# Sums on POOL in SBUF in place of identity products on PE, and norm statistics from ACT's copy, in a hybrid state-space and attention block

## The chip, the cores and the metric

One NeuronCore of a Trainium2 chip. The metric is the device time of one launch in microseconds: 11580.11 us, the median of 3 runs (11578.98 to 11580.71).

## What is computed

The input x is 8 images of 64 x 64 tokens with 96 channels, float32. Per image, cut to what matters here:

```python
x = x + ss2d(group_norm(x))                  # layer 0
t = t + attn(layer_norm(t))                  # layer 1: linear attention, N = 4096 tokens
t = t + ffn(layer_norm(t))                   # 96 -> 384 -> 96, fp8 products
# ss2d:
xh, z = split(x @ in_proj.T)                 # 192 + 192 channels
xc = silu(conv3x3(xh))
s0, s1 = xc[diag], xc[anti]                  # the tokens along two sorts of diagonals
xs = [s0, s1, reversed(s0), reversed(s1)]    # four directions
h  = h * exp(delta * A) + (delta * u) * B    # a scan over 4096 positions, 16 states n
y  = sum over n of h * C   (+ D * u)
y01 = ys[0:2] + reversed(ys[2:4])            # an end's two directions: forward plus backward
y   = y01[0][inv_diag] + y01[1][inv_anti]    # the two pairs
out = (layer_norm(y) * ln_w + ln_b) * silu(z) @ out_proj.T
```

Two sums of this are what the change is about: that of forward and backward direction (line `y01`), and that of the two pairs, diagonal and antidiagonal (the line after it).

## The kernel before, in words

**The scan.** An image is walked in 16 steps m: first pair of directions (q = 0, forward, both diagonals at once in the halves of the 128 partitions), 8 chunks of T = 512 positions, then the backward pair (q = 1), 8 chunks. A step has 16 iterations i, one for each state n; 2048 iterations in all, written out as one loop in `run`. In iteration i the engines get, each in its own order:
- ACT: `decay(i+2)` (exp, L985), jobs, `times_b(i+2)` (feedT, L1007; for one state in sixteen POOL does it, L998);
- DVE: `recur(i)`: in the five "D" states three multiplications of feed with du (L1032), then three scans (L1028), jobs between the second and the third;
- PE, in three parts: `turn(i+1)` (L1015, L1017) into the three PSUM banks `feed`, a third of `reduce(i-4)` (L1061, transposes of h that add up over the 16 states in the PSUM tile y), jobs;
- POOL: `keep(i-1)` (L1042) and `read(i-1)` (h times C, L1047), jobs;
- SP issues all DMAs in order; `fetch(i+4)` (L976) brings a C row, cc, into one of five buffers.

h has six buffers, decay three, feedT two, each feed bank one. POOL may thus be up to some three iterations behind before PE's `reduce` needs it.

**The sum of the directions.** `place(m)`, three iterations into step m+1, copies y to SBUF (ys) by ACT. For q = 0 this is one copy (L1089) and a DMA to `part` in DRAM. For q = 1 the part of the same chunk is fetched at the step's start (y0, a tile that shares its one buffer with ys, L1056), added by three PE products with the identity into y after states 8, 9 and 10 (L1074), and y then goes by two copies (L1094), one per diagonal, and eight DMAs (L1104) to `wide`, an array in DRAM from which rows of tokens can be read.

**The prologue** of step m+2 (an urgent job, L900 to L957) starts in iteration 13 of step m: products for dt, B and C, softplus (L942, with two table loads), then du = delta x u on POOL (L947, iteration 3 of step m+1), its 12 transposes on PE (L953) and three copies duT on ACT (L955). du has two buffers.

**Jobs.** What is not scan is written as Python generators: each `yield` names the engine of the next piece (act, dve, gp for POOL, pe, or bank, which also asks for one of two PSUM banks), its planned us, and a lag. `Work.at` is called at fixed places of the iteration and takes the pieces that are due, as far as a credit per engine allows; urgent jobs come first and may overdraw. The table LAGS says how many iterations after the last piece a piece is due, by the pair of engines: ACT to DVE (AV) 1, POOL to DVE (GV) 1, POOL to PE (GP) 1 and the last part. A lag in the yield replaces it: `dve(1.0, 0)` puts DVE's piece into the same iteration. Placement is fixed when the program is made; on the chip each engine runs its queue in order and waits on semaphores.

While image b is scanned, jobs do the front of image b+1 (norm, convolution: steps 0 to 5; walk: 5 to 7) and the tail of image b-1: `join` for 8 groups of 512 tokens (steps 7 to 11), `attention`, `layers` for 8 groups (12 to 15). The last image's tail stands alone at the end (`last`).
- `join(c)` loads the two pairs' rows ys[0], ys[1] from `wide`; adds them by PE products with the identity into a bank (L665), which ACT copies to yn (L672) and DVE takes the norm statistics of (L675, L676); norm, transposes, times the gate, out projection into a bank po, ACT's copy t (L708), statistics of po (L713), normed xa on POOL, its Gram matrix and transposes. At most three joins are open, and join c's sum waits for join c-2's end. In the last tail DVE adds (L656) and takes statistics from SBUF (L658).
- `layers(c)`: the same pattern with po, the copy t (L809) and statistics (L813), then the two fp8 products.

At iteration LAG + 1 = 5 of an image all jobs must be out (`work.finish(all_done)` issues what is left with no scan between), and the next image's jobs start.

Of the kernel before, what the change touches and what calls it, by code (L numbers as in the profile page):

```python
# [9 lines left out]
F32 = mybir.dt.float32  # L10
# [25 lines left out]
G = 3  # L36
# [579 lines left out]
def tail(tc, work, x, out, k, at, b, last=False):  # L616
# [4 lines left out]
    with tc.tile_pool(name=f"t1_{b}", bufs=1, **area) as p1:  # L621
# [5 lines left out]
        with tc.tile_pool(name=f"t2_{b}", bufs=8 if last else 2, **area) as p2:  # L627
# [3 lines left out]
            def join(c):  # L631
# [22 lines left out]
                if last:  # L654
                    yield dve(2.5)
                    nc.vector.tensor_tensor(yn, ys[0], ys[1], ALU.add)  # L656
                    for i in range(4):
                        nc.vector.bn_stats(st[:, i, :], yn[:, i, :])  # L658
                        nc.vector.bn_aggr(mv[:, i, :], st[:, i, :])
                for j in range(0 if last else 2):  # L660
                    ps = yield bank(0.65)
                    v = view(ps, P, 2, DI)
                    for i in range(2):
                        for d in range(2):
                            nc.tensor.matmul(  # L665
                                v[:, i, :], k.ident, ys[d][:, 2 * j + i, :],
                                start=(d == 0), stop=(d == 1), skip_group_check=True,
                            )
                        if i == 0:
                            yield pe(0.65)  # L670
                    yield act(0.5)
                    nc.scalar.copy(yn[:, 2 * j : 2 * j + 2, :], v)  # L672
                    yield dve(1.0, 0)
                    for i in range(2):
                        nc.vector.bn_stats(st[:, 2 * j + i, :], v[:, i, :])  # L675
                        nc.vector.bn_aggr(mv[:, 2 * j + i, :], st[:, 2 * j + i, :])  # L676
                    work.release(ps)
                r, m = yield from rsqrt(nc, p2, k, mv, P, 4, "n")
                yield act(1.4)
                for i in range(4):  # L680
# [27 lines left out]
                nc.scalar.copy(t, po)  # L708
                if not last:
                    nc.sync.dma_start(out=at.mid[:, s, :], in_=t)  # L710
                yield dve(1.7, 0)
                for i in range(4):
                    nc.vector.bn_stats(st[:, i, :], po[:, i, :])  # L713
                    nc.vector.bn_aggr(mv[:, i, :], st[:, i, :])
                work.release(ps)
                r, m = yield from rsqrt(nc, p2, k, mv, P, 4, "a")
                xa = ys[0].rearrange("p a c -> p (a c)")[:, 0 : 4 * (DM + 1)].rearrange("p (a c) -> p a c", a=4)
                yield gp(1.6)
# [64 lines left out]
        with tc.tile_pool(name=f"t3_{b}", bufs=8 if last else 3, **area) as p2:  # L783

            def layers(c):
# [22 lines left out]
                yield act(0.5)  # L808
                nc.scalar.copy(t, po)  # L809
                st, mv = tile("st", [P, 4, 6]), tile("mv", [P, 4, 2])  # L810
                yield dve(1.7, 0)
                for i in range(4):
                    nc.vector.bn_stats(st[:, i, :], po[:, i, :])  # L813
                    nc.vector.bn_aggr(mv[:, i, :], st[:, i, :])
                work.release(ps)
                r, m = yield from rsqrt(nc, p2, k, mv, P, 4, "f")
                xf = tile("xf", [P, 4, DM])
                yield gp(1.4)
# [41 lines left out]
def run(tc, psum, dram, x, out, w, NB):  # L860
# [39 lines left out]
    def prologue(m):  # L900
# [42 lines left out]
        w.tables()  # L943
        o.delta = delta
        yield gp(3.4)
        du = o.du = tile("du", [P, G, T])
        nc.gpsimd.tensor_tensor(du, delta, u, ALU.mult)  # L947
        duT = tile("duT", [P, TB * G, P])
        for j in range(G):
# [9 lines left out]
    def bring(m):  # L959

        b, q, c = steps[m]
        work.finish(lambda: c in image(b).walked)
        u = pool.tile([P, G, T], F32, tag="u", name=f"u_{m}", bufs=2)
        made[m] = SimpleNamespace(u=u, c={})
        for d in range(2):
            nc.sync.dma_start(
                out=u[d * GC : (d + 1) * GC],
                in_=image(b).seq[d][:, c * T : (c + 1) * T].rearrange("(g i) t -> i g t", i=GC),
            )
# [49 lines left out]
    def recur(i):  # L1019
        m, n = divmod(i, NS)  # L1020
        _, q, _ = steps[m]
        h = hs[i] = pool.tile([P, G, T], F32, tag="h", name=f"h_{i}", bufs=6)
        a = decays.pop(i)
        back = slice(None, None, -1) if q else slice(None)

        def scan(g):
            init = carry[m - 1][:, n, g : g + 1] if m % NST else 0.0
            nc.vector.tensor_tensor_scan(h[:, g, back], a[:, g, back], feed[g][:, back], init, ALU.mult, ALU.add)  # L1028

        if FEED[n] == "D":  # L1030
            for g in (1, 2, 0):
                nc.vector.tensor_tensor(feed[g], feed[0], made[m].du[:, g, :], ALU.mult)  # L1032
        scan(0)
        scan(1)
        work.at("V")
        scan(2)
# [12 lines left out]
    def reduce(i, part):  # L1049
        m, n = divmod(i, NS)  # L1050
        b, q, c = steps[m]
        if n == 0 and part == 0:
            sums[m] = psum.tile([P, TB * G, P], F32, tag="y", name=f"y_{m}")
            if q:
                other[m] = pool.tile([P, TB * 2 * DI], F32, tag="ys", name=f"y0_{m}")
                nc.sync.dma_start(out=other[m], in_=image(b).part[:, c, :])  # L1056
        y = sums[m]
        some = range(4 * part, 4 * part + 4)
        for j in some:
# [5 lines left out]
        if q and n in (1, 2, 3) and part == 2:  # L1065
            for j in range(4 * (n - 1), 4 * n):
# [2 lines left out]
                    y[:, j, :], made[m].u[:, g, r * P : (r + 1) * P], w.skip[:, g, :],  # L1069
                    start=False, stop=False, skip_group_check=True,  # L1070
                )
        if q and n in (8, 9, 10) and part == 2:
            j = n - 8
            nc.tensor.matmul(  # L1074
                y[:, 4 * j : 4 * j + 4, :].rearrange("p a c -> p (a c)"), w.ident,
                other[m][:, j * T : (j + 1) * T], start=False, stop=False, skip_group_check=True,
            )
        if part == 2:
            hs.pop(i)

    def place(m):

        b, q, c = steps[m]
        y = sums.pop(m)
        ys = pool.tile([P, TB * 2 * DI], F32, tag="ys", name=f"ys_{m}")
        if q == 0:
            nc.scalar.copy(ys, y.rearrange("p j c -> p (j c)"))  # L1089
            nc.sync.dma_start(out=image(b).part[:, c, :], in_=ys)  # L1090
            return
        rows = ys.rearrange("p (d k c) -> p d k c", d=2, k=TB)
        for d in range(2):
            nc.scalar.copy(  # L1094
                rows[:, d].rearrange("p k (g i) -> p k g i", i=GC),
                y.rearrange("p (k g) (d i) -> p d k g i", g=G, d=2)[:, d],
            )
            stride = (3 * WW + 1) * DI if d == 0 else (3 * WW - 1) * DI
            for v in range(2):
                for again in range(2):  # L1100
                    first = (c * (T // HH) + v + (again + d) * WW) * DI
                    view = image(b).wide[d][first : first + HH * stride].rearrange("(h x) -> h x", x=stride)
                    view = view[:, 0 : TB * 2 * DI].rearrange("h (k x) -> h k x", k=TB)[:, :, 0:DI]
                    nc.sync.dma_start(out=view, in_=rows[v * HH : (v + 1) * HH, d])  # L1104

    def begin(b):
        return front(tc, work, x, w, image(b), b)
# [61 lines left out]
    for i in range(total + LAG + 1):  # L1169
        m, n = divmod(i, NS)  # L1170
        b, at = divmod(i, PER)
        if i < total:
            if at == LAG + 1 and b:
                work.finish(all_done)
                work.stream(between(b))
            if at == PER // 2 and b + 2 < NB:
                work.stream(before(b + 2))
            if n == NS - 3 and m + 2 < len(steps):
                work.start(prologue(m + 2), urgent=True)
            if n == NS // 2 and m + 2 < len(steps):  # L1180
                bring(m + 2)
# [22 lines left out]
        if i + 4 < total:  # L1204
            fetch(i + 4)
        feeds.pop(i, None)

    work.finish(all_done)
    scans.close()
# [82 lines left out]
```

## Time and profile before

| what | value |
|---|---|
| runs, median of 3 | 11580.11 us |
| profiled execution | 11584.24 us, span 11582.5 us |
| mean granted TensorE clock | 0.913 |
| DVE scans L1028, 128x512 | 6144, 1263 ns (with carry) |
| POOL read L1047, 128x1536 | 2048, 3455 ns |
| POOL du L947, 128x1536 | 128, 3445 ns |
| PE L665 (a join's sum) | 896, 351 ns, busy 182.4 us |
| PE L1074 (a step's sum) | 384, 595 ns, busy 196.9 us |
| ACT copies L672, L1089, L1094 | 469, 1416, 783 ns |
| DVE statistics L675, L713, L813 | 345, 238, 237 ns |
| DMA | 1207 MB, 104 GB/s on average |

An engine's busy time is the union of its instructions; matmuls are pipelined, so 896 of 351 ns take 182.4 us. "Idle before" an instruction is the time in which its engine stood, with what released it. As each engine runs its queue in order, an instruction that waits holds up everything behind it, the scan's instructions too.

### The profile page before, as it was taken

To read this page: it belongs to the slowest core of one execution; us is meant where nothing else is said; L and a number is where in the kernel's file an instruction comes from. 1 tells how busy PE (TensorE), PEld (TensorE's weight loads), DVE (VectorE), ACT (ScalarE), POOL (GpSimd) and SP (SyncE) were. 2 spreads that over 40 slices of the span, in tenths; PEclk is the share of its full clock that TensorE was granted. 3 is DMA by queue.
4 is the path that set the end of the run, shared out by engine and by line. 5 is a ranking of instruction groups with operands and counts; after the bars stand their busy time and mean duration, and the time that the engine had idled before them with its cause. 6 is when DMAs were issued, how large, how long until landed. Compare 5 with 4: busy or idle time off the path is not lost.

```text
span 11582.5 us, 187413 instructions
## 1 busy us (share of the span) xinstructions
PE 9540.5 (82%) x63189; PEld 7973.6 (69%) x63189; DVE 9483.5 (82%) x10714; ACT 9430.0 (81%) x19571; POOL 8885.1 (77%) x6799
## 2 busy tenths in 40 slices
PE   6898889788888888888888888988889888887885
PEld 5677677676776667766677766767667676676663
DVE  2988888888878888788887888888888878888893
ACT  3888888878888888888888788887888878888883
POOL 1877887778867887777887788777887778878883
PEclk8999899898999989999899998999999889898996
DMA  3335333533335333353334433354333533332332
GB/s 91 105 91 140 100 91 91 144 107 97 98 96 134 108 105 91 106 135 104 97 98 113 125 100 104 92 133 116 100 92 98 131 107 96 100 97 86 99 97 53
DMA packets 1122757, 1207.26 MB, mean 104 GB/s; under 512 B 452789, under 2 KB 730006, under 8 KB 1121798
## 3 DMA queue, kind: packets, MB, share of 16 engines
q1 hardware_dynamic: 1121798, 1195.28, 37.6%
q8 instruction: 503, 8.24, 0.3%
q14 instruction: 456, 3.74, 0.1%
HBM read 874.83 MB, written 319.98 MB: 103 GB/s over the span
## 4 chain that ended last, share of the span: by engine, by line
PE 25%; POOL 21%; ACT 20%; DVE 15%; issue 11%; DMA 5%; SPq 3%; POOLq 0%; DVEq 0%; ACTq 0%
POOL h L1047 15%; DVE h L1028 9%; ACT feedT L1007 8%; PE y L1061 7%; PE feed L1015 6%; ACT decay L985 6%; DVE feed L1032 3%; DMA cc<-crow 3%; POOL du L947 2%; PE bank L550 2%; PE bank L915 2%; SPq L595 2%; POOL feedT L998 2%; PE bank L953 1%; POOL carry L1042 1%
## 5 line engine op out<-in xcount | busy, mean ns | idle before, releaser
L1047 POOL TENSOR_TENSOR h<-h,cc 128x1536 f32<-128x1536 f32 x2048 | 7076.9, 3455 | 368.8 <-DMA cc<-crow 187.1
L1028 DVE TENSOR_TENSOR_SCAN h<-decay,carry,feed 128x512 f32<-128x512 f32 x5376 | 6529.7, 1263 | 987.1 <-PE feed L1015 769.8
L985 ACT ACTIVATE decay<-delta,a_neg 128x512 f32<-128x512 f32 x6144 | 3971.1, 712 | 1156.1 <-DVE h L1028 1153.3
L1015 PE MATMUL feed<-ident,feedT 128*128 128x128 f32 x16896 | 3066.7, 301 | 1605.6 <-DVE h L1028 1070.5
L1061 PE MATMUL y<-ident,h 128*128 128x128 f32 x24576 | 3820.9, 288 | 127.2 <-POOL feedT L998 112.8
L1015 PEld LDWEIGHTS feed<-ident,feedT 128*128 128x128 f32 x16896 | 2178.8, 153 | 2288.1 <-ACT feedT L1007 882.8
L1007 ACT ACTIVATE feedT<-duT,rows 128x192 f32<-128x192 f32 x10240 | 3672.2, 444 | 23.8 <-PE feed L1015 21.2
L1061 PEld LDWEIGHTS y<-ident,h 128*128 128x128 f32 x24576 | 3127.9, 150 | 515.5 <-issue 335.2
L1042 POOL COPY carry<-h 128x3 f32<-128x3 f32 x2048 | 393.0, 192 | 1615.3 <-DVE h L1028 1545.8
L1032 DVE TENSOR_TENSOR feed<-feed,du 128x512 f32<-128x512 f32 x1920 | 1202.4, 687 | 137.2 <-PE feed L1017 134.6
L1028 DVE TENSOR_TENSOR_SCAN h<-decay,feed 128x512 f32<-128x512 f32 x768 | 882.5, 1201 | 127.3 <-PE feed L1015 87.5
L550 PE MATMUL bank<-wf,xp 97*128 97x192 f32 x4266 | 858.7, 332 | 0.0
L550 PEld LDWEIGHTS bank<-wf,xp 97*128 97x128 f32 x4266 | 691.0, 194 | 24.1 <-issue 13.5
L1017 PE MATMUL feed<-x,pick 77*128 77x512 f32 x1280 | 695.7, 626 | 3.4
L947 POOL TENSOR_TENSOR du<-delta,u 128x1536 f32<-128x1536 f32 x128 | 441.0, 3445 | 316.1 <-ACT delta L942 309.4
L915 PE MATMUL bank<-wx,u 128*128 128x77 f32 x3048 | 413.1, 299 | 36.2 <-DMA u<-seq 36.2
L915 PEld LDWEIGHTS bank<-wx,u 128*128 128x128 f32 x3048 | 407.3, 217 | 44.4 <-issue 39.6
L937 PE MATMUL bank<-x,ws 13*128 13x512 f32 x764 | 434.7, 649 | 1.6 <-ACT x L928 1.6
L998 POOL TENSOR_TENSOR feedT<-duT,rows 128x512 f32<-128x512 f32 x384 | 396.0, 1061 | 0.0
L955 ACT COPY duT<-bank 128x512 f32<-128x512 f32 x383 | 220.7, 576 | 176.4 <-PE bank L953 174.3
L939 DVE COPY delta<-bank 128x512 f32<-128x512 f32 x382 | 256.2, 671 | 56.4 <-PE bank L937 53.6
L1017 PEld LDWEIGHTS feed<-x,pick 77*128 77x128 f32 x1280 | 209.7, 197 | 71.7 <-DVE h L1028 39.5
(278 smaller groups left out, 7544.3 us busy)
## 6 DMA issues: line engine op xcount, KB each, us to landing
cc<-crow SPq DMA_DIRECT2D x4096, 128.0 KB
u<-seq SPq DMA_DIRECT2D x256, 384.0 KB
wide<-ys SPq DMA_DIRECT2D x512, 192.0 KB
ut<-image SPq DMA_DIRECT2D x768, 64.0 KB
seq<-us SPq DMA_DIRECT2D x128, 384.0 KB
part<-ys SPq DMA_DIRECT2D x64, 768.0 KB
y<-part SPq DMA_DIRECT2D x64, 768.0 KB
y<-wide SPq DMA_DIRECT2D x256, 192.0 KB
```

The lines of the kernel that those rows point to most:

```text
L550: nc.tensor.matmul(v[:, j, :], flat[:, o : o + P], k.wf[:, i, :], start=(i == 0), stop=(i == 8), skip_group_check=True)
L915: nc.tensor.matmul(v[:, j, :], u[:, g, j * P : (j + 1) * P], w.wx[:, q, g, :], start=(g == 0), stop=(g == G - 1))
L947: nc.gpsimd.tensor_tensor(du, delta, u, ALU.mult)
L985: nc.scalar.activation(decays[i][:, g, :], made[m].delta[:, g, :], AF.Exp, scale=w.a_neg[:, q, g, n : n + 1])
L998: nc.gpsimd.tensor_tensor(f.rearrange("p (j g) (d c) -> p g j d c", g=G, d=d)[:, g], o.duT.rearrange("p (j g) (d c) -> p g j d c", g=G, d= ...
L1007: nc.scalar.activation(f[part], o.duT[part], AF.Copy, scale=o.rows[:, j, XB + d * NS + n : XB + d * NS + n + 1])
L1015: nc.tensor.transpose(feed[g][:, j * P : (j + 1) * P], feeds[i][:, j * G + g, :], w.ident)
L1017: nc.tensor.matmul(feed[0], w.pick[:, FEED[:n].count("D"), :], made[m].x, start=True, stop=True)
L1028: nc.vector.tensor_tensor_scan(h[:, g, back], a[:, g, back], feed[g][:, back], init, ALU.mult, ALU.add)
L1032: nc.vector.tensor_tensor(feed[g], feed[0], made[m].du[:, g, :], ALU.mult)
L1047: nc.gpsimd.tensor_tensor(hs[i], hs[i], c.unsqueeze(1).to_broadcast([P, G, T]), ALU.mult)
L1061: nc.tensor.matmul(y[:, j, :], hs[i][:, g, r * P : (r + 1) * P], w.ident, is_transpose=True, start=(n == 0 and j % 4 == 0), stop=(n == NS ...
```

## The change

Four things change. (1) A join adds its two pairs in SBUF by one POOL instruction; statistics come from that sum. (2) In q = 1 steps the directions are added in SBUF by two POOL instructions, after ACT's copies, in a new urgent job `spread` which then issues the DMAs to `wide`; y0 gets a buffer of its own and is loaded at state 8; both pairs now copy y with two copies, so that `part` has the same order. (3) Statistics of t and of po are taken from ACT's copy in SBUF, with the table's lag. (4) du has one buffer, and a prologue's du waits until the last multiplication with the previous one (state 10) is in DVE's queue; the drain at an image's start is moved from iteration 5 to 7.

```diff
@@ join
                 if last:
                     yield dve(2.5)
                     nc.vector.tensor_tensor(yn, ys[0], ys[1], ALU.add)
-                    for i in range(4):
-                        nc.vector.bn_stats(st[:, i, :], yn[:, i, :])
-                        nc.vector.bn_aggr(mv[:, i, :], st[:, i, :])
-                for j in range(0 if last else 2):
-                    ps = yield bank(0.65)
-                    v = view(ps, P, 2, DI)
-                    for i in range(2):
-                        for d in range(2):
-                            nc.tensor.matmul(
-                                v[:, i, :], k.ident, ys[d][:, 2 * j + i, :],
-                                start=(d == 0), stop=(d == 1), skip_group_check=True,
-                            )
-                        if i == 0:
-                            yield pe(0.65)
-                    yield act(0.5)
-                    nc.scalar.copy(yn[:, 2 * j : 2 * j + 2, :], v)
-                    yield dve(1.0, 0)
-                    for i in range(2):
-                        nc.vector.bn_stats(st[:, 2 * j + i, :], v[:, i, :])
-                        nc.vector.bn_aggr(mv[:, 2 * j + i, :], st[:, 2 * j + i, :])
-                    work.release(ps)
+                else:
+                    yield gp(1.8)
+                    nc.gpsimd.tensor_tensor(yn, ys[0], ys[1], ALU.add)
+                    yield dve(2.1)
+                for i in range(4):
+                    nc.vector.bn_stats(st[:, i, :], yn[:, i, :])
+                    nc.vector.bn_aggr(mv[:, i, :], st[:, i, :])
...
                 nc.scalar.copy(t, po)
...
-                yield dve(1.7, 0)
+                work.release(ps)
+                yield dve(1.7)
                 for i in range(4):
-                    nc.vector.bn_stats(st[:, i, :], po[:, i, :])
+                    nc.vector.bn_stats(st[:, i, :], t[:, i, :])
                     nc.vector.bn_aggr(mv[:, i, :], st[:, i, :])
-                work.release(ps)
@@ layers: the same five lines
@@ prologue
         yield gp(3.4)
-        du = o.du = tile("du", [P, G, T])
+        while m and not made[m - 1].multiplied:
+            yield "G", 0.0, -1, False
+        du = o.du = tile("du", [P, G, T], 1)
@@ recur
+        if n == FEED.rindex("D"):
+            made[m].multiplied = True
@@ reduce
-            if q:
-                other[m] = pool.tile([P, TB * 2 * DI], F32, tag="ys", name=f"y0_{m}")
-                nc.sync.dma_start(out=other[m], in_=image(b).part[:, c, :])
+        if q and n == 8 and part == 0:
+            other[m] = pool.tile([P, TB * 2 * DI], F32, tag="y0", name=f"y0_{m}")
+            nc.sync.dma_start(out=other[m], in_=image(b).part[:, c, :])
...
-        if q and n in (8, 9, 10) and part == 2:
-            j = n - 8
-            nc.tensor.matmul(
-                y[:, 4 * j : 4 * j + 4, :].rearrange("p a c -> p (a c)"), w.ident,
-                other[m][:, j * T : (j + 1) * T], start=False, stop=False, skip_group_check=True,
-            )
@@ place
-        if q == 0:
-            nc.scalar.copy(ys, y.rearrange("p j c -> p (j c)"))
-            nc.sync.dma_start(out=image(b).part[:, c, :], in_=ys)
-            return
         rows = ys.rearrange("p (d k c) -> p d k c", d=2, k=TB)
         for d in range(2):
             nc.scalar.copy(
                 rows[:, d].rearrange("p k (g i) -> p k g i", i=GC),
                 y.rearrange("p (k g) (d i) -> p d k g i", g=G, d=2)[:, d],
             )
+        if q == 0:
+            nc.sync.dma_start(out=image(b).part[:, c, :], in_=ys)
+        else:
+            work.start(spread(m, rows), urgent=True)
+
+    def spread(m, rows):
+        b, q, c = steps[m]
+        for d in range(2):
+            yield gp(1.8, 1)
+            nc.gpsimd.tensor_tensor(
+                rows[:, d], rows[:, d], other[m].rearrange("p (d k c) -> p d k c", d=2, k=TB)[:, d], ALU.add
             )
             stride = (3 * WW + 1) * DI if d == 0 else (3 * WW - 1) * DI
...
                     nc.sync.dma_start(out=view, in_=rows[v * HH : (v + 1) * HH, d])
+        other.pop(m)
@@ the loop
-            if at == LAG + 1 and b:
+            if at == LAG + 3 and b:
+                work.finish(lambda: all_done() and not other)
                 work.finish(all_done)
                 work.stream(between(b))
...
+    work.finish(lambda: not work.urgent)
```

More of the change, by code (lines that the diff above doesn't have):

```diff
@@ L810, in layers @@
                 st, mv = tile("st", [P, 4, 6]), tile("mv", [P, 4, 2])
-                yield dve(1.7, 0)
+                work.release(ps)
+                yield dve(1.7)
                 for i in range(4):
-                    nc.vector.bn_stats(st[:, i, :], po[:, i, :])
+                    nc.vector.bn_stats(st[:, i, :], t[:, i, :])
                     nc.vector.bn_aggr(mv[:, i, :], st[:, i, :])
-                work.release(ps)
                 r, m = yield from rsqrt(nc, p2, k, mv, P, 4, "f")
@@ L963, in bring @@
         u = pool.tile([P, G, T], F32, tag="u", name=f"u_{m}", bufs=2)
-        made[m] = SimpleNamespace(u=u, c={})
+        made[m] = SimpleNamespace(u=u, c={}, multiplied=False)
         for d in range(2):
@@ L1096, in place @@
                 y.rearrange("p (k g) (d i) -> p d k g i", g=G, d=2)[:, d],
+            )
+        if q == 0:
[8 more added lines that the diff above has]
+                rows[:, d], rows[:, d], other[m].rearrange("p (d k c) -> p d k c", d=2, k=TB)[:, d], ALU.add
             )
```

## The prediction

> **What bounds the kernel now.** I read the page's part 1, then the busy times of single steps (a step is 16 iterations, one for each state), then the waits by pair, and last the order of time around the costliest of the waits that the change touches.
>
> ```profile
> PE 9540.5 (82%) x63189; PEld 7973.6 (69%) x63189; DVE 9483.5 (82%) x10714; ACT 9430.0 (81%) x19571; POOL 8885.1 (77%) x6799
> ```
>
> Four engines stand within five points of each other, so no share decides. The stretches differ, however: a step of image 3 with joins, one with layers, and a step of image 7 in which no job runs (PE, PEld, DVE, ACT, POOL busy, then clock, DMA):
>
> ```profile
> 5162.80:5258.70 95.90, 78.82 (x569) 66.57 (x569) 78.64 (x107) 75.23 (x164) 73.30 (x75) 0.96 0.46 122
> ...
> 5435.80:5524.50 88.70, 71.48 (x473) 57.07 (x472) 75.23 (x94) 76.26 (x162) 75.75 (x72) 0.92 0.36 99
> ...
> 10959.00:11034.20 75.20, 62.50 (x412) 51.80 (x411) 68.60 (x67) 65.62 (x139) 64.28 (x36) 0.91 0.35 100
> ```
>
> The bare step is DVE's: 68.6 of 75.2 us (91%). The join step has only 82% of DVE, and no engine above that: it loses 17 us to waits in queues that run in order. Three pairs of the list of waits are the statistics' own:
>
> ```profile
> DVE st L713 <- ACT t L708: 135.8, 37, 11.8
> ...
> DVE st L675 <- ACT y L672: 109.5, 74, 5.2
> ...
> DVE st L813 <- ACT t L809: 71.7, 31, 12.1
> ```
>
> The batch statistics read the same PSUM bank as ACT's copy and start only when the copy has ended. They are issued with lag 0, in the iteration of the copy, and stand between two scans in DVE's queue. At 5180 us the copy is behind softplus, two table loads, feedT and ys:
>
> ```profile
> 5185.34 0.46 ACT L708 COPY t<-bank 128x384 f32<-128x384 f32 x1
> 5185.83 0.27 DVE L713 BATCH_NORM_STATS2 st<-bank 128x6 f32<-128x96 f32 x1 [3.61 <-ACT t L708]
> ...
> 5187.33 3.59 DVE L1028 TENSOR_TENSOR_SCAN h<-decay,carry,feed 128x512 f32<-128x512 f32 x3
> ...
> 5188.63 0.66 PE L1015 MATMUL feed<-ident,feedT 128*128 128x128 f32 x4 [3.44 <-DVE h L1028]
> ...
> 5188.67 1.96 ACT L985 ACTIVATE decay<-delta,a_neg 128x512 f32<-128x512 f32 x3 [2.87 <-DVE h L1028]
> ```
>
> DVE stood 3.61 us, then PE 3.44 and ACT 2.87 for the scan behind it: all lose it at once. POOL is seldom late for anyone here. In the chain of this window its read (L1047) is not among the twelve largest lines, and L665 has 2.7%. The chain of the bare step gives L1047 44.5%, but it enters POOL where y (L1061) starts 0.1 us after the second feedT of POOL; ACT's ys copy ends there too, and where the two ends part (step 14 of an image) y starts with ACT's. I don't build on POOL's 21% of the page's chain.
>
> **The change, part by part** (against the profiled execution: 11584.24 us, span 11582.5; the runs' median is 11580.11, 4 less, so I take differences off the median).
>
> *Statistics of t and po (L713, L813).* Same 64+64 groups, now from SBUF, one iteration later, so that the copy is an iteration (4 to 6 us) old. The waits are 135.8 and 71.7; of these 24.9 and 12.1 lie in the last image's end, after the scans, where no scan is behind them. 110.9+59.6 = 170 us of stalls of the scan go. Where would they go instead? ACT or PE are next, but they stood too. I take nine tenths: **-153**. The bank is given back in the same iteration as before. Each job gets an iteration longer; image 3's last job ends at step 15, iteration 9, 12 iterations before the next image's point, so nothing is drained there (moving that point two iterations on costs nothing, as long as this room stands).
>
> *A join's sum.* Of 56 joins, each loses 16 PE passes (L665: 896 instructions, 182.4 us busy, 3.3 us a join), two ACT copies (112 x 469 ns) and the wait at L675. It gains one POOL addition of 128x768: between L854 (384 elements, 914 ns) and L947 (1536, 3445 ns) this is 1.76 us. The Trainium skill speaks against it (GPSIMD Engine Reference, Engine selection: elementwise work of two inputs belongs on VectorE, about twice as fast). The row agrees: DVE's own addition of this size (L656) takes 958 ns. By the rule the new 56+128 additions would cost 176 us of DVE, the engine that is at 91% in a bare step; on POOL they cost 184 x 1.76 = 324 us, and POOL goes to 9209 us, 80% of the span. As POOL idles 11 us in a bare step and 22 in the join step, I take POOL's side: mostly covered.
> L675's 109.5 us go, but the statistics now wait, an iteration later, for POOL. POOL starts a read 0.3 us after its scan when level; read and addition take 5.2 us, and DVE comes to the place some 7.5 us after that scan. So about 2 us are spare when POOL is level, and POOL is 2 to 8 us behind in a third of the iterations. Bounds 0 and 3 us a join; I take 1: 56. Net **-54**. PE's products are on the path for 2.7% of 98 us and two joins, 1.3 us a join, 73 us; with the copies' part and something next in line, **-65**.
>
> *A step's sum in the second walk pair (64 steps).* PE loses 384 passes, 196.9 us busy (3.1 us a step, iterations 12 to 14); POOL gains 3.5 us a step in iterations 4 and 5. The wide DMAs are now queued behind these additions in SP's queue, 8 x 0.63 us, and cc fetches behind them; a fetch is for four iterations on, so some 4 us later is hidden. y0's load now has its own tile: the wait L1056 (40 us of SP) was not on the path. In a first-pair step the copy becomes two: 1.47 us for the pair against 1416 ns, 64 x 0.05 = **+3**. The last step's additions stand before the last tail: **+3**.
>
> *du with one buffer.* du (3445 ns) is held from iteration 3 to 10, until DVE has used the old one. This leaves POOL level at 3 (it read 8.0 us late there, du and three feedT before it), which pays for the 3.5 us of additions at 4 and 5. Its 12 transposes go from iterations 4-6 to 11-13, and three ACT copies from 5-7 to 12-14. There ACT has no gap in a bare step (10929.8 to 10950.2); a copy adds some 0.48 us, so feedT of 14 and 15 come 0.5 and 1 us later. In second-pair steps the PE time is exchanged with the products that go (3 x 0.43 against 3 x 0.44) and two gaps of DVE (0.3 and 0.8 us at 6 and 7) close: -0.6 a step; in first-pair steps nothing is given back: +0.9. 64 x 0.3 = **+20** (bounds -70 and +110).
> The new wait: PE's transposes of du are behind POOL. PE comes there 8 us after read 9 ends in most steps, du needs 3.5. In image 3's steps 12, 14 and 0 PE comes 3.2 us after, 0.9 after and 0.6 before (with 3.1 of other POOL work in step 12), so PE, and feed behind it, would stand 3.5, 2.6 and 4.1; the last less 3.4 for the du that has left iteration 3. 6.8 an image, 8 images: **+54** (bounds 0, and 3.4 us in every job step).
>
> *A fuller POOL.* PE and ACT already wait for POOL's small results (L681 14.1, L727 5.8+6.5, L825 5.3+7.3 us). With a third to a half of its idle time in these steps gone they double, less where the copies no longer come between: **+25**. The Trainium skill (SBUF — State Buffer, "two separate sides") says that a DVE instruction in a 2-port mode and a POOL one exclude each other for a whole instruction. This row shows it:
>
> ```profile
> L840 DVE CAST hq<-h x64: 932/1763/3960, 2692.6 to 11563.5; 128x1536 fp8e5<-128x1536 f16 x64
> ```
>
> From 932 to 3960 ns for the same cast. If the statistics, now in SBUF, fell under the rule, each could wait for a 3.45 us read: 736 of them at 1 us each and the change would lose. But L658, which reads SBUF, takes 335 ns against 345 of L675 from PSUM: no faster mode, so no lock. I take the row, and **+8** for hq alone (113.7 us, POOL 7% busier there).
>
> Sum: -153 -54 -65 +3 +3 +20 +54 +25 +8 = -159. 11580 - 159 = **11420**.
>
> **The rivals.** (A) As above, 0.60: 11420, from 11290 to 11540 by the bounds.
> (B) POOL becomes the engine that is waited for, 0.18, slower. Place: PE's transposes of du at iteration 11. It decides from the point where POOL is over 4 us behind its scans at iteration 9 in the job steps (8 to 15 and 0: 9 of 16, some 68 in all). Price: a whole du each, 68 x 3.45 = 235 us above my sum: 11580 - 159 + 235 = 11655. For: POOL gains 3.5 to 7.4 us in just these steps, PE is in order. Against: in image 3 POOL was less than 3 us behind at 9 in six of these nine.
> (C) Everything given back, 0.14: steps 7 to 11 fall to DVE's busy time at the bare step's 91%. The join step: 78.6/0.91 = 86.4 against 95.9; over image 3's five such steps 40 us, and 15 in the layer steps: 55 x 7 = 385: 11195.
> (D) It does little, 0.08: DVE's stalls are taken up by PE's feed (DVE already waits 857 us for L1015): 11575.
>
> **How the numbers follow.** Within 0.2% (11557 to 11603, about what a measurement of this kernel can tell from no change) lie D and a little of A and B. Faster 0.74, same 0.08, slower 0.18. Range 11230 to 11600: it leaves out most of B and half of C.
>
> **What would show it.** The three pairs DVE st <- ACT gone from the waits, and in their place DVE st <- POOL y of some 56 us; PE bank <- POOL du of some 54; the join step near 88 us with DVE at 89%; the bare step within 1 us of 75.2; POOL at 80%, its read still 3.45 us. Wrong, if PE or ACT wait for POOL for over 200 us in all, if the bare step is over 77, or if image boundaries show a drain.

## The result, and the profile after

The changed kernel takes 11443.49 us (median of 4 runs, 11435.44 to 11459.93) against 11579.55 us before (4 runs, 11561.34 to 11580.71): a ratio of 0.9888, 95% interval 0.9871 to 0.9905. It is 1.1% faster. The forecast was 11420. The number is close, but by luck: the experiments below show that it came about by two large errors of opposite sign.

The profiled execution took 11445.95 us, its span 11444.1. Busy times of the engines:

```profile
PE 9310.8 (81%) x61909; PEld 7836.7 (68%) x61909; DVE 9464.3 (83%) x10714; ACT 9376.6 (82%) x19523; POOL 9230.9 (81%) x6983
```

PE has lost 1280 passes and 230 us, POOL has gained 346 us (324 were forecast), DVE's work is the same within 19 us. The same three stretches as before: step 9 of image 3 (joins), step 12 of that image (layers), and the bare step of image 7 (start and end, length, then PE, PEld, DVE, ACT, POOL busy, granted TensorE clock, DMA share, GB/s):

```profile
5088.50:5189.70 101.20, 85.97 (x543) 72.95 (x543) 80.17 (x109) 75.14 (x165) 81.63 (x85) 0.82 0.44 113
5369.90:5470.80 100.90, 78.36 (x487) 64.97 (x486) 82.37 (x102) 77.99 (x169) 76.70 (x71) 0.86 0.32 86
10825.30:10898.90 73.60, 59.65 (x405) 50.42 (x404) 68.22 (x67) 65.48 (x139) 67.72 (x38) 0.89 0.36 101
```

The bare step is 73.6 us against 75.2, with 3.4 us more of POOL: covered, as forecast, and shorter by more than the 1 us allowed. The join step is not at 88 us with DVE at 89%; it has become longer, 101.2 against 95.9, and the layer step 100.9 against 88.7. Read the clock column: 0.82 in place of 0.96, 0.86 in place of 0.92. PE is busy for 86.0 us with 543 matmuls where 569 took 78.8.

The waits by pair (us in total, times, longest):

```profile
DVE h L1016 <- PE feed L1003: 870.8, 701, 6.6
...
DVE delta L925 <- PE bank L923: 147.9, 97, 19.1
...
DVE st L662 <- POOL y L659: 65.1, 24, 5.4
PE bank L941 <- POOL du L935: 53.8, 23, 5.5
```

The two new waits stand where the prediction put them, near its sizes (56 and 54 us). The three waits of the statistics for ACT are gone but for 23.7 and 15.9 us in the last image's end. Yet from the start to the last scan DVE's idle time fell from 1904 only to 1787 us, though the pairs for ACT had held 280 of it: 65 us are the new wait for POOL, and delta's wait for PE rose from 54 to 148. One sign that the prediction had named as speaking against it is met, barely: summed over the list of waits, PE and ACT wait for POOL for 184 and 25 us, 209 together, where it drew the line at 200 (before: 153 and 14).

Where the time went, from the first read on POOL of one step to that of the next, in the two profiled executions (their spans differ by 138 us): image 0 is 30 us shorter (no join or layer runs there), images 1 to 5 only 7 to 17 each, image 6 33 and image 7 15. In images 1 to 5 the steps 5 to 8 together gain 24 us an image, steps 13 and 14 gain 14, and step 12 alone loses 12.

### The profile page after: what moved, and what is told of

It reads as the page before. It is cut to its first block, busy times and chain, and to the rows that moved or that the text cites. A ratio compares the mean times of both kernels' runs of the same rounds, so it can differ in the third digit from the quotient of the medians.

```text
span 11444.1 us, 184841 instructions
## 1 busy us (share of the span) xinstructions
PE 9310.8 (81%) x61909; PEld 7836.7 (68%) x61909; DVE 9464.3 (83%) x10714; ACT 9376.6 (82%) x19523; POOL 9230.9 (81%) x6983
## 4 chain that ended last, share of the span: by engine, by line
PE 26%; ACT 21%; POOL 16%; DVE 15%; issue 10%; DMA 8%; SPq 4%; POOLq 0%; DVEq 0%; ACTq 0%
POOL h L1037 10%; DVE h L1016 9%; ACT feedT L995 9%; PE y L1051 7%; PE feed L1003 6%; ACT decay L973 6%; DMA cc<-crow 4%; DVE feed L1020 4%; PE bank L550 3%; SPq L595 2%; PE bank L901 2%; PE feed L1005 1%; POOL du L935 1%; PE bank L923 1%; DMA y<-wide 1%
## 5 line engine op out<-in xcount | busy, mean ns | idle before, releaser
L1037 POOL TENSOR_TENSOR h<-h,cc 128x1536 f32<-128x1536 f32 x2048 | 7080.2, 3457 | 512.4 <-DMA cc<-crow 311.6
L1003 PE MATMUL feed<-ident,feedT 128*128 128x128 f32 x16896 | 3110.5, 305 | 1623.6 <-DVE h L1016 1050.2
L1051 PE MATMUL y<-ident,h 128*128 128x128 f32 x24576 | 3866.6, 291 | 132.0 <-issue 61.6
L1003 PEld LDWEIGHTS feed<-ident,feedT 128*128 128x128 f32 x16896 | 2227.7, 156 | 2231.7 <-ACT feedT L995 1026.7
L1051 PEld LDWEIGHTS y<-ident,h 128*128 128x128 f32 x24576 | 3174.8, 152 | 521.5 <-issue 419.4
L1032 POOL COPY carry<-h 128x3 f32<-128x3 f32 x2048 | 418.0, 204 | 1166.5 <-DVE h L1016 1053.0
L901 PE MATMUL bank<-wx,u 128*128 128x77 f32 x3048 | 361.5, 276 | 0.0
L901 PEld LDWEIGHTS bank<-wx,u 128*128 128x128 f32 x3048 | 353.7, 193 | 1.6 <-ACT duT L943 0.2
L941 PE MATMUL bank<-ident,du 128*128 128x128 f32 x1532 | 241.2, 282 | 54.0 <-POOL du L935 53.8
```

What stands on the lines that cost most here:

```text
L901: nc.tensor.matmul(v[:, j, :], u[:, g, j * P : (j + 1) * P], w.wx[:, q, g, :], start=(g == 0), stop=(g == G - 1))
L1003: nc.tensor.transpose(feed[g][:, j * P : (j + 1) * P], feeds[i][:, j * G + g, :], w.ident)
L1037: nc.gpsimd.tensor_tensor(hs[i], hs[i], c.unsqueeze(1).to_broadcast([P, G, T]), ALU.mult)
L1051: nc.tensor.matmul(y[:, j, :], hs[i][:, g, r * P : (r + 1) * P], w.ident, is_transpose=True, start=(n == 0 and j % 4 == 0), stop=(n == NS ...
```

## The experiments

Differences in us are the ratio's share of the 11575 us that the kernel before took beside these runs (11571 to 11575); brackets are 95% intervals. Where a wait or a step is named, it is that of one profiled execution. First each part alone.

**Part 3 alone** (statistics of t and po from ACT's copy, with the lag), run e1_stats:

```diff
-                yield dve(1.7, 0)
+                work.release(ps)
+                yield dve(1.7)
                 for i in range(4):
-                    nc.vector.bn_stats(st[:, i, :], po[:, i, :])
+                    nc.vector.bn_stats(st[:, i, :], t[:, i, :])
                     nc.vector.bn_aggr(mv[:, i, :], st[:, i, :])
-                work.release(ps)
... (the same in layers)
```

> The kernel before with the third part of the change alone: the statistics of t and of po come from ACT's copy in SBUF, one iteration later. Theory A (the stalls of DVE behind ACT's copy are the gain): the waits of DVE at L713 and L813 vanish in the scans, about -150 us, 11430. Theory B (the gain is PE's relief from the identity products): nothing, 11580. Theory C (every edit shifts where the jobs fall, and the gain is the sum of such shifts): anything within 60 us of the kernel before, with the two waits gone and others grown by as much.

Measured: ratio 1.0019 (1.0012 to 1.0027), 22 us slower. The 170 us of stalls are gone, and nothing is gained. Three waits before, then the same three in this run:

```profile
DVE h L1028 <- PE feed L1015: 857.3, 739, 10.9
...
DVE delta L939 <- PE bank L937: 53.6, 42, 19.8
```

```profile
DVE h L1028 <- PE feed L1015: 959.3, 783, 10.0
...
DVE st L675 <- ACT y L672: 185.5, 81, 4.2
...
DVE delta L939 <- PE bank L937: 79.0, 60, 19.4
```

Before, the join's wait (L675) was 109.5. The three rose by 102, 76 and 25 us, 203 together; DVE's idle time to the last scan went from 1904 to 1913 us. The stall did not vanish, it moved to the next places where DVE meets ACT (the join's sum) and PE (feed). PE had a share in this. Its busy time in this run:

```profile
PE 9638.3 (83%) x63189; PEld 8052.8 (69%) x63189; DVE 9496.4 (82%) x10714; ACT 9426.0 (81%) x19571; POOL 8891.3 (77%) x6799
```

The same 63189 products took 9540.5 us before: 98 us less, with 2015 us at half of TensorE's clock against 2139 here. This run alone does not tell how much of the lost gain is the ring of waits and how much the slower clock; e5_no_stats below, where PE's busy time hardly differs, tells more.

**Part 1 alone** (POOL adds the two pairs in a join), run e2_join:

> The kernel before with the join's sum alone: POOL adds the two pairs in SBUF, statistics from that sum. Theory A: -54 for the waits at L675 less new waits for POOL, -65 for PE, some +15 for a fuller POOL: about -105 us, 11475. Theory B: PE loses 182 us busy, -100 to -180. Theory C: within 60 us of the kernel before.

Measured: 0.9935 (0.9923 to 0.9947), 75 us faster, between theory C's 60 and theory A's 105. Step 9 of image 3 in this run:

```profile
5125.00:5214.60 89.60, 73.91 (x545) 62.07 (x545) 80.17 (x110) 73.06 (x160) 78.36 (x77) 0.98 0.52 139
```

This is the join step that was forecast for the whole change: 89.6 us, DVE 80.17 of it (89%). The clock is 0.98.

**Parts 2 and 4 together** (the step's sum on POOL, du with one buffer, the drain two iterations later), run e3_step_du, and **part 4 alone**, run e4_du:

> The kernel before with the sum of the directions on POOL, du in one buffer and the drain two iterations later; joins and statistics as before. Theory A: +20 for the moved transposes and copies, +54 for PE's wait for du, +6 for copies and the end, some +10 for POOL: +90 us, 11670. Theory B: PE loses 197 us busy, -50 to -150. Theory C: within 60 us; the image without a tail gains, as it did in the whole change (image 0, 30 us less).

> The kernel before with du in one buffer alone (du waits for the last multiplication with the one before it, iteration 10 in place of 3). Theory A: in first-pair steps +0.9 us, in second-pair steps +0.6 (the identity products stay, so PE's time is not exchanged), and PE's wait for du: about +120 us, 11700. Theory C: within 60 us; POOL is level at iteration 3 and the bare step keeps its 75 us.

Measured: 0.9958 (0.9946 to 0.9970) and 0.9986 (0.9980 to 0.9993), 49 and 16 us faster where 90 and 120 slower were expected. In e4_du image 0 is 31 us shorter. In images 1 to 5 the steps 5 to 8 gain 23 us an image, and the steps 11 to 15 lose 22 (step 11 alone 12). The scans' waits for ACT fell from 142 to 21 us, and those for PE's feed from 857 to 785. The parts' sum is +22 - 75 - 49 = -102, the whole -130.

**The whole without part 3**, run e5_no_stats:

```diff
+                yield dve(1.7, 0)
+                for i in range(4):
+                    nc.vector.bn_stats(st[:, i, :], po[:, i, :])
+                    nc.vector.bn_aggr(mv[:, i, :], st[:, i, :])
                 work.release(ps)
-                yield dve(1.7)
-                for i in range(4):
-                    nc.vector.bn_stats(st[:, i, :], t[:, i, :])
-                    nc.vector.bn_aggr(mv[:, i, :], st[:, i, :])
... (the same in layers)
```

> The changed kernel without part 3: statistics of t and of po again from the PSUM bank, in the iteration of ACT's copy (lag 0). Theory A (my prediction's term, each removed stall of DVE is worth nine tenths of itself): 153 us are given back, 11595 us. Theory B (part 3 does nothing wherever it stands, as alone, where it cost 22 us): 11443 - 22, 11420 us. Theory C (alone its gain went into the wait for ACT's copy of a join's sum, 77 us more there; with the join on POOL that place is gone, so the part is worth the 34 us by which the whole beats the sum of its parts): about 11475 us. In the trace: DVE st <- ACT t and <- ACT of the layers' t are back, some 170 us before the last scan; under B the wait of the scans for PE's feed falls by about as much.

Measured: 11440.31 us, 0.9889 (0.9874 to 0.9904): the changed kernel's time, to within the 26 us that the two intervals leave. Theory A is out by 155 us; the run lies between B's 11420 and C's 11475, nearer to B. Within the whole, part 3 is worth nothing that can be measured. Here PE's busy time is the same, 9313.7 us against 9310.8, so no slower products hide a gain. Its waits:

```profile
DVE h L1016 <- PE feed L1003: 801.8, 692, 5.3
...
DVE st L699 <- ACT t L694: 136.6, 41, 11.8
...
DVE st L799 <- ACT t L795: 48.3, 21, 12.1
...
PE bank L941 <- POOL du L935: 15.9, 14, 3.5
```

Most of the stalls are back (148 of 170 us ahead of the last scan), and feed's wait is 69 us shorter than in the changed kernel, delta's 30, that for POOL's sum 38. Parts 1, 2 and 4 add up here: -75 - 49 = -124 against -128.

**The changed kernel with lag 0**, still from SBUF, run e6_lag0:

> The changed kernel with the statistics of t and po from ACT's copy in SBUF, but in the copy's own iteration (lag 0 in place of the table's 1). Theory A: it is the lag that takes the stall away, so DVE waits 170 us for ACT's t again: 11443 + 150 = 11595 us. Theory B: the stalls move between DVE's places and sum to the same: within 20 us of 11443. Theory D (the lag itself costs, because the twelve statistics groups of three jobs then fall into one stretch of step 12, which got 11.7 us longer): step 12 goes back, some 8 x 11 us gained, 11360 us. The source alone (SBUF for PSUM) should move nothing: statistics of 227 ns either way.

Measured: 0.9912 (0.9899 to 0.9926), 28 us above the changed kernel's ratio (give or take 25). Not A's 150 and not D's gain, and a little outside B's 20: step 12 does give its 12 us back, but step 9 becomes 15 us longer than before in place of 3.

**du early, its transposes late**, on the kernel before, run e7_duT_late:

```diff
         du = o.du = tile("du", [P, G, T])
         nc.gpsimd.tensor_tensor(du, delta, u, ALU.mult)
+        while m and not made[m - 1].multiplied:
+            yield "G", 0.0, -1, False
         duT = tile("duT", [P, TB * G, P])
... (and the flag `multiplied`, set as in the change)
```

> The kernel before with du on POOL at iteration 3 as before and two buffers, but its twelve transposes on PE and three copies duT on ACT held until state 10's multiplication is in DVE's queue, as in the run with one du buffer (which took 11558, 16 less than before). Theory ACT (that run gained because the three duT copies left the iterations in which softplus and its table loads hold ACT up): the same gain, and more by the 54 us of PE's wait for POOL's du, which is now long done: 11575 - 16 - 40 = 11520 us. Theory POOL (it gained because du left POOL's iteration 3): no gain, 11575 to 11590 us. My prediction had POOL's side only: at best 0.

Measured: 0.9996 (0.9987 to 1.0004), no difference. Image 0 gains 35 us as in e4_du, so that gain belongs to the transposes and copies (ACT and PE), not to POOL. In images 1 to 5 it is as there too: steps 5 to 8 gain 23 us an image, steps 11 to 15 lose 22. The scans' waits for ACT fell to 19 us and those for PE's feed to 728, more than in e4_du, and the run is not faster for it. The 11 us to e4_du lie at the edge of both intervals; what du's leaving iteration 3 is worth to POOL is not settled.

**The join's sum on DVE**, run e8_join_dve (as it differs from e2_join):

```diff
-                    yield gp(1.8)
-                    nc.gpsimd.tensor_tensor(yn, ys[0], ys[1], ALU.add)
-                    yield dve(2.1)
+                    yield dve(3.0)
+                    nc.vector.tensor_tensor(yn, ys[0], ys[1], ALU.add)
```

> Part 1 alone, but with the join's addition on DVE in place of POOL, in one piece with the statistics. The Trainium skill's rule (elementwise work of two inputs belongs on VectorE, about twice as fast as GpSimd): DVE's 0.96 us takes the place of POOL's 1.82 us and of DVE's wait for it: 11490 us or below, at least as good as POOL's 11501. My theory (DVE is the engine nearest to its bound, POOL has room): 56 x 0.96 = 54 us more on DVE's path than with POOL: 11501 + 48 = 11549 us.

Measured: 0.9991 (0.9983 to 0.9999). On DVE the sum gains 10 us, on POOL 75; both forecasts (11490 and 11549 us) were too fast. The groups of this run, the sum in the walk and in the last image's end (mean ns of one after the bar):

```profile
L659 DVE TENSOR_TENSOR y<-y,y 128x768 f32<-128x768 f32 x56 | 112.4, 2007 | 0.0
...
L656 DVE TENSOR_TENSOR y<-y,y 128x768 f32<-128x768 f32 x8 | 7.7, 958 | 46.6 <-DMA y<-wide 46.6
```

The same instruction takes 2007 ns on average beside POOL's reads and 958 after them; POOL needs 1820 ns. So within this walk VectorE is not even faster at this addition. Two single ones on the timeline (start, us, what it is):

```profile
3874.41 3.44 POOL L1032 TENSOR_TENSOR h<-h,cc 128x1536 f32<-128x1536 f32 x1
3874.63 4.04 DVE L659 TENSOR_TENSOR y<-y,y 128x768 f32<-128x768 f32 x1
...
5230.14 0.95 DVE L659 TENSOR_TENSOR y<-y,y 128x768 f32<-128x768 f32 x1
```

The first starts 0.22 us into a read (L1032 here) and ends 0.82 us after it; the second has no read beside it. Of the 56 additions in the walk 38 start within a read, and every one ends 0.81 to 0.82 us after that read's end. The other 18 take 0.93 to 0.95 us; within one of them a read starts, and this read takes 4.14 us in place of 3.46. So the two exclude each other: whichever starts first runs to its end. The hq casts before keep to the same: 40 of 64 start within a 3.45 us operation of POOL, and all 40 end 0.81 to 0.83 us after it.

**The kernel before without the statistics of t and po**, run e9_no_tpo, with the order of all else kept:

> The kernel before with the statistics of t and of po left out (the norms then take the join's own statistics, and ones for the layers; the order of everything else is unchanged). This takes away the 170 us for which DVE stands behind ACT's copy in the walk and some 215 us of DVE's own work (512 statistics of 238 ns, 512 aggregates of 182 ns). Theory A (DVE's queue is the path in the job steps): 11575 - 300, about 11275 us. Theory B (the path turns through ACT and PE there, and DVE's stall is only where it meets their lateness; the run with the stalls gone was 22 us slower): the stalls are worth nothing, and of the work a part: 11575 - 215 x 0.5, between 11425 and 11520 us, and DVE's wait for PE's feed rises by 70 us or more over 861.

Measured: 0.9860 (0.9845 to 0.9875), 162 us faster, a little more than B's range (55 to 150) and little over half of A's 300. Its busy times:

```profile
PE 9544.2 (83%) x63189; PEld 7974.9 (70%) x63189; DVE 9325.2 (82%) x9754; ACT 9418.1 (82%) x19571; POOL 8892.2 (78%) x6799
```

DVE's busy time fell by 158 us (the 215 us of the expectation add up instructions that overlap), while its idle time to the last scan stayed, 1895 us against 1904: its wait for PE's feed rose by 66 us, that for ACT's y by 47. So about as much came off the total as came off DVE's work, and the 170 us of stalls again count for nothing. Read together with e1_stats, it is DVE's work that is on the path here, not its waiting; no run took the work away and left the stalls.

**Only the wait of a join's sum removed**, run e10_join_wait (statistics from ACT's copy with the lag, PE's products kept), and **one product in place of two** (one of the two pairs is left out of the sum), run e11_one_product:

```diff
-                        for d in range(2):
-                            nc.tensor.matmul(
-                                v[:, i, :], k.ident, ys[d][:, 2 * j + i, :],
-                                start=(d == 0), stop=(d == 1), skip_group_check=True,
-                            )
+                        nc.tensor.matmul(
+                            v[:, i, :], k.ident, ys[0][:, 2 * j + i, :],
+                            start=True, stop=True, skip_group_check=True,
+                        )
```

> The kernel before with one thing changed in a join's sum: its statistics come from ACT's copy in SBUF with the table's lag, products on PE and copies on ACT as they were. This takes the 109.5 us of DVE's wait for ACT's y away and nothing else. Theory A: 11575 - 100 = 11475 us. Theory B (what was found for t and po holds here too): within 25 us of 11575, on either side, and the gain of the join on POOL (74 us) is then that of PE's products and ACT's copies.

> The kernel before with one product with the identity in a join's sum in place of two (one of the two pairs is left out of the sum): 448 of 896 PE instructions go, some 91 us of PE's busy time; ACT's copies and DVE's wait stay. If PE's products are what the join on POOL saved: half of 74 or more, 11575 - 40 = 11535 us. If it was the wait of DVE or the copies of ACT: within 15 us of 11575.

Measured: 0.9990 (0.9982 to 0.9998), 12 us for a wait of 109.5; and 0.9971 (0.9960 to 0.9982), 34 us for half of the products. In e10_join_wait DVE stands as long as before (1902 us to the last scan); the waits for ACT turn up at the layers and for PE at feed:

```profile
DVE h L1028 <- PE feed L1015: 893.4, 761, 10.8
...
DVE st L813 <- ACT t L809: 126.0, 44, 11.9
```

The layers' wait was 71.7 before. So the join's gain on POOL is in the main that of PE's products, not of the wait. What ACT's two copies a join add (51.8 us of its time in all) was not tried by itself.

**Part 3 for the joins only, within the whole**, run e12_mix:

> The changed kernel with statistics from ACT's copy and the lag for the joins' t only; the layers' po again from the PSUM bank with lag 0. Theory B: the part is worth nothing in either place, 11443 within 15 us. Theory D (the lag costs where the layers' groups meet in step 12, 11.7 us longer in the changed kernel and 1.2 shorter with lag 0; and it pays in step 9, 3.1 us longer against 12.8): both good halves, some 6 x 10 us: 11385 us.

Measured: 0.9960 (0.9947 to 0.9972), 83 us slower than the changed kernel. Neither theory has this. With the lag in the joins, the layers' statistics begin at iteration 10 of step 12 instead of 8 (e5_no_stats). Two jobs then stand side by side: image 3 has sixteen statistics and aggregates in one iteration of step 12, as the changed kernel and e1_stats have too (all three have a step 12 that is 10 to 12 us longer than before), and again in one iteration of step 14, where the changed kernel has eight in each of two. Steps 14 and 15 are 8 and 5 us longer than in the changed kernel. That this pairing is the cause is read off the order of the instructions; it was not tried by itself. No run that computes the same beats the changed kernel measurably; e5_no_stats equals it.

## Why the prediction was right in its number and half wrong in its reasons

| term | predicted | measured |
|---|---|---|
| statistics of t and po | -153 | +22 alone (14 to 31), within the whole 0 (give or take 26) |
| a join's sum | -54 - 65 | -75, with its load on POOL |
| a step's sum, du, drain | +3 +3 +20 +54 | -49, with its load on POOL |
| fuller POOL, hq | +25 +8 | in the two lines above |
| all | -159 | -130 |

**The step that failed** is the first term: "110.9+59.6 = 170 us of stalls of the scan go. Where would they go instead? ACT or PE are next, but they stood too. I take nine tenths". The observation at 5185 us was right, the inference was not. Scan, decay, feedT and feed form a ring over DVE, ACT and PE: each waits for the one before it. That all three stand while DVE waits does not mean that time is lost there: if DVE doesn't wait at this place, it waits for ACT's or PE's lateness a few instructions later. e1_stats and e10_join_wait remove 170 and 110 us of waits, and DVE's idle time to the last scan is 1913 and 1902 us against 1904. As DVE's work hardly changes in these two, this is the total told in another way; what the traces add is where the waits went (feed, the join's sum, the layers). Rival D named this ("DVE's stalls are taken up by PE's feed"); it holds for part 3, not for the whole. The test that a wait must pass is not its length but what becomes of the total.

**The join.** PE's products: half of them give 34 us, so some 67 for all by doubling (an estimate), where -65 was forecast: right, as far as the estimate goes. The wait: 12 us for removing it, where the sum had 109.5 less 56: wrong by the same error as above. The choice of POOL was right, against the Trainium skill's rule of engine selection (GPSIMD Engine Reference): by the rule e8_join_dve should have been the faster of the two, and it gives 10 us against 75. The prediction still priced DVE at 958 ns, from a row of the last image's end, where POOL is idle. In the walk it is 2007: 56 of them take 112 us in place of 54. These 58 us are most of the 65 between the two runs (an estimate, which holds if all of DVE's time counts, as in e9_no_tpo). The skill's page that the prediction cites for hq (SBUF — State Buffer) lets the exclusion hold for DVE instructions with two SBUF inputs as well, which this addition has; the prediction left that half of the rule out. The 38 additions that end 0.82 us after a read agree with it. The statistics have one input and do not show it (L662 takes 333 ns beside POOL), as was said.

**du and the step's sum.** The sign is wrong. The wait of PE for POOL's du is 53.8 us, forecast 54; its price is nil as far as these runs tell: e5_no_stats has 15.9 us of it and the time of the whole. Rival B, which put 235 us more on it, is out. The +20 was read off bare steps of image 7 and carried over to all. There it is about right (in e4_du its steps 10 to 15 change by -0.1 to +1.0 us each), but image 0 gains 31 us, and in images 1 to 5 the steps 5 to 8 gain what the steps 11 to 15 lose. What gains in the former is not shown: it would fit that transposes and copies left the iterations in which softplus and its table loads make ACT late, as the scans' waits for ACT fell from 142 to 21 us; but e7_duT_late has that fall too and no gain in all. The step's sum (with the later drain) is worth e3 less e4, -33 us, about the -30 that lies between the two expectations.

**POOL** runs at 81%, forecast 80; its read stays at 3457 ns; the sum of 128x768 takes 1820 ns (estimate 1760); hq rose by 6.5 us, forecast 8.

**The join step that did not come.** With part 1 alone it is the one predicted; with all parts it is 101.2 us. Rival C, which saw every such step near 86 us, falls with it. The same step in images 1 to 6:

| kernel | step 9, us | granted clock |
|---|---|---|
| before | 95.4 to 97.0 | 0.88 to 0.96 |
| e2_join | 88.5 to 90.5 | 0.94 to 1.00 |
| e9_no_tpo | 92.2 to 93.9 | 0.93 |
| e10_join_wait | 85.1 to 87.1 | 0.90 to 0.96 |
| after | 94.6 to 101.2 | 0.82 to 0.91 |
| e5_no_stats | 102.6 to 112.8 | 0.77 to 0.90 |

One step alone misleads, as jobs fall into other steps when the order changes: e10_join_wait has the shortest step 9, but its step 11 is 11 us longer than before. In the last two of these kernels, with the same products in the same order in images 1 to 5, the longer of these steps are those with the lower clock: in e5_no_stats 102.6 us at 0.90 and 112.2 at 0.77, in the changed kernel 94.6 at 0.91 and 101.2 at 0.82. Where the steps differ less it need not be so: e3_step_du has 95.8 at 0.88 and 98.0 at 0.90. On PE's own rows, just ahead of this step in the changed kernel (start, us, then what it is, and the idle time before it):

```profile
5075.51 0.60 PE L1003 MATMUL feed<-ident,feedT 128*128 128x128 f32 x4
...
5082.97 0.63 PE L1003 MATMUL feed<-ident,feedT 128*128 128x128 f32 x4 [1.43 <-DVE h L1016]
...
5084.21 1.06 PE L1003 MATMUL feed<-ident,feedT 128*128 128x128 f32 x4
...
5088.26 1.11 PE L1003 MATMUL feed<-ident,feedT 128*128 128x128 f32 x4 [2.13 <-DVE h L1016]
```

The same four products take 0.60 us and, from 5083.5 on, 1.06: the clock records have 0.5 for 27.3 us from there. All records of the trace are 0.5 or 1.0 and last multiples of 3.41 us (but for the last, which ends with the record). Cut into such windows, of those at full clock in which PE was busy for under 40%, every one is followed by a window at half clock (192 of 192 before, 210 of 210 after, from the first scan to the last); of those with over 90% none is (of 1544 and 1419); between 60% and 80% it is about one in ten. The Trainium skill (TensorE: Matmul & The Clock Gate, Part 1) has the same window and the two states, and puts the fall after an idle window; here under 40% busy is idle enough. Time at half clock in all: 2015 us before, 2246 after. Over steps 7 to 11 of images 1 to 6 part 1 alone gains 26 us an image at a mean clock of 0.93, the whole 12 at 0.885: about 15 an image are missing. It would fit that part of what was gained is given back by a PE that stands idle in longer pieces and is then slow. It is not the amount of PE's work that decides: e11_one_product takes 448 products away and has 1977 us at half clock, e1_stats takes none away and has 2139. How much is cause and how much effect (a step that stands longer has a lower clock too) is not settled; no run kept PE busy to hold its clock.

## What to carry to other kernels

In a loop whose engines wait for each other in a ring, a stall is no gain in waiting: take the wait away by itself and see what becomes of the total before you add it to a sum; here stalls of 170 and of 110 us were worth +22 and -12 when removed, while half of the join's products taken off PE gave half of what was forecast for all, and 158 us of DVE's work (with 170 of its stalls) gave 162. Read the granted clock of the very step beside its length: a change that bunches PE's idle time can go with half of the clock in the stretches where PE is needed. Price an operation by a row from the stretch in which it will run, not from one where its neighbour is idle.

## What the runs showed of the hardware

- DVE's addition of 128x768 in SBUF takes 958 ns alone and 2007 ns on average (up to 4.1 us) beside POOL's 3.45 us reads; POOL's own takes 1820. An addition that starts within a read ends 0.81 to 0.82 us after it (38 of 38).
- TensorE's clock went to one half for at least 3.41 us after every such window in which PE was busy for under 40%; the changed kernel has 18 more of these windows between the first and the last scan and 231 us more at half clock.
- Batch statistics take the same time from SBUF (333 ns for 192 columns, 230 for 96) as from PSUM (345, 238), beside a busy POOL too.
